# Recorded order for three engines in the middle slots of a deformable bottleneck, two images per statistics instruction, and a norm's scale in two halves

## The chip, the cores and the metric

The kernel runs on one core of a Trainium2 chip. The metric is the device time of one execution in microseconds. Three runs of the kernel before took 2812.07, 2812.46 and 2814.18 us; the median is 2812.46 us.

## What is computed

Two layers follow each other on 64 images of 1024 channels and 14 x 14 pixels. The first is a bottleneck of three convolutions with batch norms. The second, in which the change lies, is a bottleneck whose middle convolution samples its input at learned offsets:

```python
out = conv(x, w1)                                          # 1024 -> 256, 1x1
out = relu(group_norm(out, gn1_scale, gn1_bias))           # 32 groups per image
om = conv(out, w_off, pad=1) + b_off                       # 27 channels, 3x3
off_x, off_y, mask = om[:, :9], om[:, 9:18], sigmoid(om[:, 18:])
sampled = bilinear_sample(out, grid_y + off_y, grid_x + off_x) * mask
out = einsum('bckhw,ock->bohw', sampled, w2)               # 256 -> 256, 9 taps
out = relu(group_norm(out, gn2_scale, gn2_bias))
out = conv(out, w3)                                        # 256 -> 1024, 1x1
out = group_norm(out, gn3_scale, gn3_bias)
return relu(out + x)
```

A group norm takes mean and variance of each image over the pixels and the channels of a group (8 channels in the first two norms, 32 in the third).

## The kernel before, in words

Everything is float32. Channels lie on the 128 partitions, in blocks of 128: 8 blocks of the 1024 channels (`CB`), 2 of the 256 (`MB`). The images are worked on in pairs; a pair's block is a tile of 128 x 392, image 0 in the first 196 columns and image 1 in the last. There are 32 pairs (`NP`).

**Slots.** The second layer is a pipeline over pairs. `slot(t)` (a function inside `build_second_bottleneck`) traces, woven into one list of steps, work on several pairs: `first_conv(t + 1)` (products named d, line 1095), its norm and the offset convolution (om, line 1191) with `selection(t + 1)`, which takes the sigmoid mask (line 1230) and bounces offsets and mask through DRAM; `factors(t + 1)`, the interpolation weights; `transposes(t + 1)`; `sampling(t, e)` (sp, line 1416), bilinear sampling as products with a matrix S, in two halves e of five and four taps; `second_conv(t, e)` (pd, line 1528), 63 products as a sevenfold scheme with sums between them; `second_norm(t - 1)`, `third_conv(t - 1)` (d with 196 columns, line 1665), `third_norm(t - 1)`, and the sum with the input, relu and store, `output`, of pair t - 1's first half of blocks and of pair t - 2's second half. `residual(t + 2)` finishes the first layer's last sum for a later pair. A slot begins with 16 products of `first_conv`; then `sp[0]` is woven with the first half of `third_conv`, then come two of its steps, om and `selection`, then `sp[1]` woven with the rest of `third_conv`, then pd of both halves. Before the first slot `fill` does the work of the first pairs, and after the last `tail` finishes pair 31.

**Who sets the order.** Each engine runs its instructions in the order in which they stand in its stream. With `tc.manual_schedule(engines=...)` an engine's stream is the order of tracing. In the slots before, only TensorE (PE) is in that set. The streams of VectorE (DVE), ScalarE (ACT), GpSimd (POOL) and of the DMA queue on SyncE (SP) are laid by the framework's planner, which picks among what it holds to be ready. An instruction under `tc.keep_in_program_order` stays behind the one traced before it on its engine. The planner also chooses which free buffer a tile gets.

**Buffers.** In PSUM the pool `ps` has three banks (d, transposes), `ps_s` has three (sampled tiles, two tiles of pd), `ps_d` holds `pd0` and `pd1`. A sampled tile `pt` is copied to SBUF by ScalarE (line 1424), which frees its bank. In SBUF, tag `sm0` or `sm1` (one buffer each) holds first X, the factor by columns, and later the sampled taps of the same half. `corners(t, e)` (line 1396) multiplies S by X on VectorE.

**Norms.** `Norm.stats` (line 1004) takes the statistics of a block. BATCH_NORM_STATS2 gives count, mean and sum of squares separately for its even and its odd elements. `total` transposes them, so that channels lie along the free axis, `mean` sums over groups (lines 1025 to 1036), `root` clamps on VectorE (line 1041) and takes the power -0.5 on GpSimd (line 1042), `scale` transposes back (line 1048) and makes the factors `sc` and `sh` (lines 1057 to 1063). `third_norm`'s last step `end` then issues 16 ScalarE activations (line 1733), one for each block and image.

Other lines that the prediction names: 216 and 228, sum and relu of `residual`; 795, a sum of the first layer; 1206 to 1218, the end of the offset convolution (an activation, then sums into `off`); 1257 and 1264, sum and product of `factors`; 1167, four sums of `transform` after a relu (line 1126); 1484, the subtractions between products of pd; 1552 to 1568, `E`, `V` and `h2` at the end of pd; 1672 to 1685, the same for `third_conv`.

Of the kernel before, what the change touches and what calls it, by code (L numbers as in the profile page):

```python
# [10 lines left out]
FP = mybir.dt.float32  # L11
AF = mybir.ActivationFunctionType
# [4 lines left out]
P = 128  # L17
# [3 lines left out]
CB = 8  # L21
# [23 lines left out]
def kernel(  # L45
# [879 lines left out]
    def build_second_bottleneck(l1, path, run, early):  # L925
# [48 lines left out]
        sets = {}  # L974
        for n in (MB, CB):
            sets[n] = [
                one.tile([P, 10 * n + Q], FP, tag=f"st{n}_{m}", name=f"st{n}_{m}_{run}") for m in range(2)
            ]
            for t in sets[n]:
                nc.gpsimd.memset(t, 0.0)  # L980

        class Norm:
# [3 lines left out]

            def __init__(self, nb, size, scol, bcol, name, b0=0):
                self.nb, self.name, self.b0 = nb, name, b0  # L990
                self.scol, self.bcol = scol + b0, bcol + b0
                self.ng, self.n = Q // size, 2 * size
                self.R = None

                kind = MB if nb <= MB else CB
                self.U = 2 * kind
                sets[kind].append(sets[kind].pop(0))
                self.st = sets[kind][-1]
                self.kind = kind

            def stats(self, b, src):
                rows = self.st[:, : 6 * self.U].rearrange("p (s u) -> p s u", s=6)
                for i in range(2):
                    last = nc.vector.bn_stats(rows[:, :, 2 * b + i], src[:, ts(i, HW)])  # L1004
                return last

            def groups(self, v):

                return v.rearrange("p (g n) -> p g n", g=self.ng)

            def total(self):
                self.R = one.tile([P, 2, Q, 2], FP, tag="nR", name=self.name + "R")
                st, U = self.st, self.U
                squares = bass.AP(st.tensor, st.offset + U, [st.ap[0], (3 * U, 2), (U, 2), (1, Q)])
                nc.vector.transpose(self.R.rearrange("p m c e -> p e m c"), squares)

            def mean(self):
                if self.R is None:
                    self.total()
                self.G = small.tile([P, 2, 4], FP, tag="nG", name=self.name + "G")  # L1020
                total, var = (self.G[:, m, : self.ng] for m in range(2))
                D = one.tile([P, 2 * Q], FP, tag="nD", name=self.name + "D")
                means, squares = (self.R[:, m].rearrange("p c e -> p (c e)") for m in range(2))

                nc.vector.tensor_reduce(total, self.groups(means), mybir.AxisListType.X, ALU.add)
                nc.vector.scalar_tensor_tensor(
                    self.groups(D),
                    total.unsqueeze(2).to_broadcast([P, self.ng, self.n]),
                    -1.0 / self.n,
                    self.groups(means),  # L1030
                    ALU.mult,
                    ALU.add,
                )
                nc.vector.tensor_tensor(D, D, D, ALU.mult)
                nc.vector.scalar_tensor_tensor(D, squares, 2.0 / HW, D, ALU.mult, ALU.add)
                nc.vector.tensor_reduce(var, self.groups(D), mybir.AxisListType.X, ALU.add)

            def root(self):

                v = self.G[:, 1, : self.ng]  # L1040
                nc.vector.tensor_scalar(v, v, 0.0, self.n * EPS, ALU.max, ALU.add)
                nc.gpsimd.tensor_tensor(v, v, mhalf[:, : self.ng], ALU.pow)

            def scale(self, tie=lambda v: v):
                nb, U = self.nb, 2 * self.nb
                B = small.tile([P, 2, Q], FP, tag="nB", name=self.name + "B")
                G = self.G[:, :, : self.ng].unsqueeze(3).to_broadcast([P, 2, self.ng, Q // self.ng])
                tie(nc.vector.transpose(B, G))
                self.sc, self.sh = (
                    small.tile([P, self.kind, 2], FP, tag=f"g{v}{self.kind}", name=self.name + v)[:, :nb]  # L1050
                    for v in ("sc", "sh")
                )
                mean, root = (B[:, m, :U].rearrange("p (b i) -> p b i", i=2) for m in range(2))
                gamma, beta = (
                    vec[:, c : c + nb].unsqueeze(2).to_broadcast([P, nb, 2]) for c in (self.scol, self.bcol)
                )
                nc.vector.scalar_tensor_tensor(
                    self.sc, root, self.n**0.5, gamma, ALU.mult, ALU.mult
                )
                nc.vector.scalar_tensor_tensor(  # L1060
                    self.sh, mean, -1.0 / self.n, self.sc, ALU.mult, ALU.mult
                )
                nc.vector.tensor_tensor(self.sh, self.sh, beta, ALU.add)  # L1063
# [558 lines left out]
        def z_of(p, b):  # L1622


            return pairs[p]["z"][b % 2][:, b // 2]
# [94 lines left out]
            order += [(o, c) for o in range(len(first), CB) for c in range(MB)]  # L1720
            return [lambda a=a: step(*a) for a in order]

        def third_norm(p):
            q = pairs[p]

            def end():
                n = q["gn3"][0]

                n.scale(tc.keep_in_program_order)
                for b in (0, 2, 4, 6, 1, 3, 5, 7):  # L1730
                    z = z_of(p, b)
                    for i in range(2):
                        nc.scalar.activation(  # L1733
                            z[:, ts(i, HW)],
                            z[:, ts(i, HW)],
                            AF.Identity,
                            bias=n.sh[:, b, i : i + 1],
                            scale=n.sc[:, b, i : i + 1],
                        )

            return [
                lambda: q["gn3"][0].total(),
                lambda: q["gn3"][0].mean(),
                lambda: q["gn3"][0].root(),
                end,
            ]

        def output(p, m):

# [42 lines left out]
        def weave(a, b):  # L1792

            both = [((n + 0.5) / len(l), m, s) for m, l in enumerate((a, b)) for n, s in enumerate(l)]
            return [s for _, _, s in sorted(both, key=lambda v: v[:2])]
# [19 lines left out]
        def slot(t):  # L1815
# [21 lines left out]
            )  # L1837
            weights = [lambda e=e: corners(t, e) for e in range(2)] if this else []

            late = [lambda: output(t - 2, 1)] if t >= 2 else []  # L1840

            loads = [lambda: load(t + 2)] if t + 2 < NP and not (early and t < 1) else []
            if this and not d1 and not early:
# [61 lines left out]
            todo += put(pd[E - 1], [s for _, s in extra], [k for k, _ in extra])  # L1905
            if ahead:
                todo.append(lambda: list(spread_columns(t + 1, 1)))
            for step in todo:
                step()

# [94 lines left out]
        with tc.manual_schedule(engines={mybir.EngineType.PE}):  # L2005
            if early:
                fill()
            for t in range(0 if early else -2, NP):
                slot(t)
                if t == NP - 2:  # L2010
                    reach()
# [86 lines left out]
```

## Time and profile before

| | |
|---|---|
| median of the runs | 2812.46 us |
| profiled execution | 2814.81 us, its span 2812.9 us |
| granted TensorE clock, mean | 0.992 |
| from 1100 to 2669 us (slots 2 to 29): TensorE busy | 1568.95 of 1569.00 us |
| VectorE, ScalarE, GpSimd busy in it | 1344.76, 933.13, 387.30 us |

The profile has one row per group of instructions: line, engine, operation, what it writes and reads, shapes, the count, then busy time in us and mean duration in ns, then the idle time of the engine before it and what ended it. A timeline has start and duration in us, the engine, and the same names; in brackets is the idle time before and its releaser. In a table by stretches each pair is busy us and, in brackets, the number of instructions, for TensorE's matmuls, its weight loads, VectorE, ScalarE and GpSimd, then the granted clock and the DMAs. Ends of matmuls are modelled, so for TensorE the distance from start to start says more than the duration. The outer parts of the second layer look different from its middle; here is TensorE's share of the time in stretches of 20 us near the end:

```profile
2700.00:2720.00 20.00, 20.00 (x119) 19.15 (x118) 15.11 (x36) 11.55 (x27) 2.71 (x3) 1.00 0.26 76
2720.00:2740.00 20.00, 15.02 (x59) 9.95 (x57) 13.12 (x30) 8.09 (x16) 2.83 (x3) 0.83 0.61 207
2740.00:2760.00 20.00, 18.88 (x89) 14.78 (x90) 11.82 (x32) 8.54 (x21) 6.95 (x12) 1.00 0.13 41
2760.00:2780.00 20.00, 20.00 (x62) 11.59 (x61) 11.94 (x32) 10.64 (x21) 1.57 (x2) 1.00 0.27 80
2780.00:2800.00 20.00, 11.97 (x35) 6.10 (x33) 14.16 (x60) 6.37 (x14) 2.12 (x3) 0.92 0.01 3
```

### The profile page before, as it was taken

How to read it: one execution, taken by the hardware profiler on the slowest of the kernel's cores; microseconds unless marked ns; L12 is line 12 of the kernel's file. 1: busy time of each engine (PE TensorE's matmuls, PEld its weight loads, DVE VectorE, ACT ScalarE, POOL GpSimd, SP SyncE). 2: the span in 40 equal slices, each digit the busy share in tenths (PEclk: the TensorE clock that was granted, in tenths of full speed). 3: DMA queues.
4: the chain of work that ended last, by engine and by line, in shares of the span. 5: the costliest groups of instructions: out<-in, count | busy, mean ns of one | idle time of the engine just before them, and what ended most of it. 6: DMA issues, size and time to landing. Idle time of an engine off the chain costs nothing.

```text
span 2812.9 us, 39819 instructions
## 1 busy us (share of the span) xinstructions
PE 2753.4 (98%) x12930; PEld 2012.7 (72%) x12930; DVE 2372.3 (84%) x5284; ACT 1323.8 (47%) x2723; POOL 936.1 (33%) x1069
## 2 busy tenths in 40 slices
PE   9999899998999989999999999999999999999996
PEld 5555555554555567887888788878887888788874
DVE  7877899998888878888888888888888888888876
ACT  0000221212555545565556555655565556555654
POOL 4630366663666302222221222122212222222221
PEclk9999999999999999999999999999999999999998
DMA  7666000003555544555455545554555455546541
GB/s 229 195 175 172 27 1 0 1 1 131 210 204 212 183 132 149 167 181 192 152 172 177 191 151 177 175 194 146 183 174 192 143 191 167 191 143 193 168 141 52
DMA packets 350318, 424.21 MB, mean 151 GB/s; under 512 B 27892, under 2 KB 292500, under 8 KB 349844
## 3 DMA queue, kind: packets, MB, share of 16 engines
q1 hardware_dynamic: 350100, 421.57, 46.0%
q8 instruction: 104, 1.70, 0.3%
q14 instruction: 114, 0.93, 0.1%
HBM read 296.49 MB, written 116.76 MB: 147 GB/s over the span
## 4 chain that ended last, share of the span: by engine, by line
PE 59%; DVE 2%; DMA 1%; issue 1%; SPq 1%; ACT 0%; POOL 0%; ACTq 0%; POOLq 0%; DVEq 0%
PE pd L1528 22%; PE sp L1416 13%; PE d L1095 10%; PE d L1665 10%; PE om L1191 2%; PE tr L1294 1%; DMA X<-wd 1%; PE pd L1447 1%; DMA S<-wd 0%; DVE st L1004 0%; SPq L1379 0%; SPq L1335 0%; DVE z L1771 0%; DVE S L1396 0%; ACT h L1580 0%
## 5 line engine op out<-in xcount | busy, mean ns | idle before, releaser
L1416 PE MATMUL sp<-S,aT 126*128 126x420 f32 (+3 forms) x1536 | 487.2, 415 | 8.1 <-DVE S L1396 5.6
L1528 PE MATMUL pd<-sm,w2b_sb 128*128 128x196 f32 x2232 | 400.6, 329 | 0.0
L1424 ACT COPY sm<-sp 128x336 f32<-128x336 f32 (+3 forms) x640 | 285.7, 452 | 220.8 <-PE sp L1416 196.9
L1528 PEld LDWEIGHTS pd<-sm,w2b_sb 128*128 128x128 f32 x2232 | 371.3, 190 | 0.0
L534 PE MATMUL c<-v,u_sb 128*128 128x392 f32 x1024 | 343.0, 497 | 10.6 <-DVE bn1sh L167 8.2
L1095 PE MATMUL d<-h,w1b_sb 128*128 128x392 f32 x1024 | 343.9, 493 | 3.9 <-ACT h L228 3.9
L534 PEld LDWEIGHTS c<-v,u_sb 128*128 128x128 f32 x1024 | 194.6, 191 | 159.0 <-DVE v L520 11.7
L1528 PE MATMUL pd<-sm,Sc 128*128 128x196 f32 x1674 | 308.1, 329 | 0.0
L1095 PEld LDWEIGHTS d<-h,w1b_sb 128*128 128x128 f32 x1024 | 193.1, 190 | 140.1 <-ACT h L228 8.0
L1484 DVE TENSOR_TENSOR sm<-sm 128x980 f32<-128x980 f32 (+2 forms) x257 | 268.4, 1055 | 20.1 <-PE pd L1528 8.8
L1528 PEld LDWEIGHTS pd<-sm,Sc 128*128 128x128 f32 x1674 | 278.7, 190 | 0.2
L1416 PEld LDWEIGHTS sp<-S,aT 126*128 126x128 f32 x1536 | 258.4, 191 | 20.9 <-issue 9.7
L1733 ACT ACTIVATE z<-z,gn_0sh,gn_0sc 128x196 f32<-128x196 f32 x496 | 222.5, 537 | 44.6 <-DVE gn_0sh L1063 44.6
L1559 POOL TENSOR_TENSOR E<-V,E 128x196 f32<-128x196 f32 x31 | 18.6, 601 | 543.5 <-DVE V L1558 543.5
L520 DVE TENSOR_TENSOR v<-t 128x392 f32<-128x392 f32 x256 | 193.0, 812 | 0.0
L1665 PE MATMUL d<-h,w3b_sb 128*128 128x196 f32 x744 | 174.0, 329 | 0.8 <-ACT h L1580 0.8
L1665 PEld LDWEIGHTS d<-h,w3b_sb 128*128 128x128 f32 x744 | 133.6, 189 | 51.6 <-issue 19.1
L1758 ACT ACTIVATE z<-z 128x784 f32<-128x784 f32 x124 | 102.7, 853 | 133.0 <-DVE z L1756 132.9
L1677 POOL TENSOR_TENSOR E<-V,E 128x196 f32<-128x196 f32 x124 | 74.2, 598 | 265.5 <-DVE V L1672 265.5
L1396 DVE TENSOR_TENSOR S<-S,X 126x840 f32<-126x840 f32 (+1 forms) x192 | 148.4, 824 | 10.6 <-DMA X<-wd 10.4
L389 PE MATMUL c<-xc,w1a_sb 128*128 128x392 f32 x384 | 149.1, 497 | 5.6 <-DMA xc<-in_x_dram 5.6
L1004 DVE BATCH_NORM_STATS2 st<-z 128x6 f32<-128x196 f32 x496 | 151.6, 352 | 3.2
(684 smaller groups left out, 4967.6 us busy)
## 6 DMA issues: line engine op xcount, KB each, us to landing
xc<-in_x_dram SPq DMA_DIRECT2D x128, 392.0 KB
h<-o SPq DMA_DIRECT2D x64, 784.0 KB
h<-in_x_dram SPq DMA_DIRECT2D x64, 784.0 KB
h<-h SPq DMA_DIRECT2D x64, 784.0 KB
out_dram<-z SPq DMA_DIRECT2D x124, 392.0 KB
X<-wd SPq DMA_DIRECT2D x64, 413.4 KB
S<-wd SPq DMA_DIRECT2D x64, 413.4 KB
S<-wd SPq DMA_DIRECT2D x64, 330.8 KB
```

The costliest lines, as they stand in the source:

```text
L389: nc.tensor.matmul(acc[m], a, b, start=(j == 0), stop=(j == HB - 1))
L520: nc.vector.tensor_tensor(v[:, u].rearrange("p (i y x) -> p i y x", y=7, x=7), cols[c][:, :, i : i + 13 : 2, :], cols[c][:, :, j : j + 13 ...
L534: nc.tensor.matmul(m[u], u_sb[:, c, u, k % 4, ts(o, P)], vts[k][c][:, u], start=(c == 0), stop=(c == MB - 1),)
L1004: last = nc.vector.bn_stats(rows[:, :, 2 * b + i], src[:, ts(i, HW)])
L1095: nc.tensor.matmul(q["pt"][o], w1b_sb[:, c, ts(o, P)], q["y"][:, c, :], start=(c == 0), stop=(c == CB - 1),)
L1396: nc.vector.tensor_tensor(S[:, piece], S[:, piece], X(piece), ALU.mult)
L1416: nc.tensor.matmul(pt[:, i], q["aT"][:, i0 + i, c, starts.index(r0), :], q["S"][e][g, r0][:, :, i0 + i, :], start=(j == 0), stop=(j == len ...
L1424: nc.scalar.copy(dst, pt.rearrange("p i k n -> p k i n"))
L1484: return nc.vector.tensor_tensor(dst, a, b, ALU.subtract)
L1528: nc.tensor.matmul(bank[:, m % 2], a[:, k], b[:, k - k0],  start=(k == 0 and m in (5, 0, 2, 6)), stop=(k == T - 1), skip_group_check=True,)
L1665: nc.tensor.matmul(bank[:, m % 2 if m < 6 else 1], a, b, start=(m < 6), stop=True, skip_group_check=True)
L1733: nc.scalar.activation(z[:, ts(i, HW)], z[:, ts(i, HW)], AF.Identity, bias=n.sh[:, b, i : i + 1], scale=n.sc[:, b, i : i + 1],)
```

## The change

There are three parts. First, slots 2 to 29 (counted from 0) are traced by a new function `steady`, in a block that adds VectorE, GpSimd and ScalarE to the engines in recorded order. SP stays with the planner, and TensorE's order is the one that `slot` gives. Second, `third_norm(p, False)` makes the factors but issues only the eight activations of one half of the blocks; the other eight are issued by `scaled(p, 1)` in the next slot, ahead of `output(p, 1)`. Third, `Norm.stats` takes both images of a block with one instruction, reading their elements alternately, so that even elements are image 0 and odd ones image 1. The layout of sums follows: the groups of both images lie side by side, and in the first two norms (2 blocks of 4 groups) the transpose back is done before the power instead of after it. The third part also holds for the slots outside `steady`, for `fill` and for `tail`.

```diff
             def stats(self, b, src):
                 rows = self.st[:, : 6 * self.U].rearrange("p (s u) -> p s u", s=6)
-                for i in range(2):
-                    last = nc.vector.bn_stats(rows[:, :, 2 * b + i], src[:, ts(i, HW)])
-                return last
+                return nc.vector.bn_stats(rows[:, :, b], src.rearrange("p (i q) -> p q i", i=2))
...
-            def root(self):
-
-                v = self.G[:, 1, : self.ng]
+            def spread(self, tie=lambda v: v):
+                B = small.tile([P, 2, 2, Q], FP, tag="nB", name=self.name + "B")
+                G = self.G[:, :, : 2 * self.ng].unsqueeze(3).to_broadcast([P, 2, 2 * self.ng, self.n])
+                tie(nc.vector.transpose(B, G))
+                self.B = B[:, :, :, : self.nb]
+
+            def root(self, tie=lambda v: v):
+
+
+                if self.nb < self.ng:
+                    self.spread(tie)
+                    v = self.B[:, 1]
+                else:
+                    v = self.G[:, 1:, : 2 * self.ng]
+                half = mhalf[:, : v.shape[1] * v.shape[2]].rearrange("p (a b) -> p a b", a=v.shape[1])
                 nc.vector.tensor_scalar(v, v, 0.0, self.n * EPS, ALU.max, ALU.add)
-                nc.gpsimd.tensor_tensor(v, v, mhalf[:, : self.ng], ALU.pow)
+                nc.gpsimd.tensor_tensor(v, v, half, ALU.pow)
...
-        def third_norm(p):
+        def third_norm(p, both=True):
             q = pairs[p]
 
             def end():
-                n = q["gn3"][0]
-
-                n.scale(tc.keep_in_program_order)
...
+                q["gn3"][0].scale(tc.keep_in_program_order)
+                for m in range(2 if both else 1):
+                    scaled(p, m)
...
+        def scaled(p, m):
+
+            q = pairs[p]
+            n = q["gn3"][0]
+            if m in q.setdefault("scaled", set()):
+                return
+            q["scaled"].add(m)
+            for b in range(m, CB, 2):
+                z = z_of(p, b)
+                for i in range(2):
+                    nc.scalar.activation(
...
-            late = [lambda: output(t - 2, 1)] if t >= 2 else []
+            late = [lambda: scaled(t - 2, 1), lambda: output(t - 2, 1)] if t >= 2 else []
...
+        def steady(t):
+
+
+            sp = [sampling(t, e) for e in range(2)]
+            pd = [second_conv(t, e) for e in range(2)]
+            d1, d3 = first_conv(t + 1), third_conv(t - 1)
+            norm1, norm2, norm3 = first_norm(t + 1), second_norm(t - 1), third_norm(t - 1, False)
+            distances, end = factors(t + 1)
+            half = len(d3) // 2
...
+            todo = at(
+                d1,
+                ((0,), [lambda: scaled(t - 2, 1)]),
+                ((1, 1, 7, 9, 9, 10, 10, 10), norm2),
+                ((6,), [lambda: output(t - 2, 1)]),
+                ((10,), [lambda: corners(t, 0)]),
+            )
+            todo += at(weave(sp[0], d3[:half]), ((4, 4, 8, 14, 16, 18, 21), norm1))
+            todo += [lambda: corners(t, 1)] + d3[half : half + 2]
+            todo += offset_conv(t + 1) + selection(t + 1) + [lambda: load(t + 2)]
+            todo += weave(sp[1], d3[half + 2 :])
+            todo += at(
+                pd[0],
+                ((1, 1, 1, 9), norm3),
+                ((5, 20), [lambda e=e: first_sum(t, e) for e in range(2)]),
+                ((6, 11, 16, 21), transposes(t + 1)),
+                ((6, 13), [distances, end]),
+                ((21,), [lambda: residual(t + 2)]),
+            )
+            todo += [lambda: list(spread_rows(t + 1, 0)), lambda: list(spread_columns(t + 1, 0))]
+            todo += [lambda: list(spread_rows(t + 1, 1)), lambda: lend(t + 1)]
+            todo += at(pd[1], ((16,), [lambda: output(t - 1, 0)]))
+            todo.append(lambda: list(spread_columns(t + 1, 1)))
+            for step in todo:
+                step()
...
-            for t in range(0 if early else -2, NP):
+            middle = range(2, NP - 2) if early else range(0)
+            for t in range(0 if early else -2, middle.start):
+                slot(t)
+            with tc.manual_schedule(
+                engines={
+                    mybir.EngineType.DVE,
+                    mybir.EngineType.Pool,
+                    mybir.EngineType.Activation,
+                }
+            ):
+                for t in middle:
+                    steady(t)
+            for t in range(middle.stop, NP):
                 slot(t)
```

In `at(steps, (places, extras), ...)` an extra step is traced just ahead of the step with the given number.

## The prediction

> **What bounds the kernel now.** I read the page's busy row first, then the busy time by stretches over the slots that the change rewrites (slot t starts with the first product of `first_conv(t + 1)`, line 1095; slots 2 to 29 run from about 1100 to 2669 us), then TensorE's waits, then the timeline of one slot, the one that starts at 1828.6 us.
>
> ```profile
> PE 2753.4 (98%) x12930; PEld 2012.7 (72%) x12930; DVE 2372.3 (84%) x5284; ACT 1323.8 (47%) x2723; POOL 936.1 (33%) x1069
> ```
>
> ```profile
> 1100.00:2669.00 1569.00, 1568.95 (x8902) 1295.98 (x8901) 1344.76 (x3304) 933.13 (x1986) 387.30 (x532) 1.00 0.53 173
> ```
>
> The second line is the stretch of the 28 slots, and TensorE (the first pair of numbers in it) is busy in it for 1568.95 of 1569.00 us at the full granted clock. Asked for the stretch from 1156 to 2669 us, the table of waits has not one row for PE; VectorE has 86%. The starts of slots are 56.04 to 56.07 us apart (56.35 the first time). Busy could still hide slack, so I looked at start to start: a 196-column product takes two records 0.166 us apart wherever it stands. The slots are bound by TensorE's own instructions. The change keeps their number and order (`steady` weaves d1, sp, d3, om, transposes and pd as `slot` does), so it can shorten nothing there. It can only open gaps, or move something at the edges (fill, slots 0, 1, 30, 31, tail), where TensorE does wait.
>
> **The parts, one by one.**
>
> Statistics: per slot 24 BATCH_NORM_STATS2 on 196 elements become 12 on 392, whose two images are read alternately, 784 bytes apart.
>
> ```profile
> L1004 DVE BATCH_NORM_STATS2 st<-z 128x6 f32<-128x196 f32 x496 | 151.6, 352 | 3.2
> ...
> L586 DVE BATCH_NORM_STATS2 st<-h 128x6 f32<-128x392 f32 x64 | 34.6, 555 | 0.0
> ```
>
> The old ones follow each other every 0.27 us, so a block costs 0.54. A contiguous 392 takes 0.555 us, and as neighbours overlap by about 0.08, it costs 0.475. Gain 0.07 x 12 = 0.8 us of VectorE a slot, off the path. [...] But line 216 reads its operand `r` in just this way (two streams alternately, also 784 bytes apart) and takes 623 ns, where line 795, also three operands of 392, without the jump, takes 625. I take the row: 0.555. [...]
>
> Norm: the transpose in `spread` handles 128 instead of 64 elements, 312 instead of 238 ns by lines 1015 and 1048: +0.075 x 3 = 0.2 us a slot. `root` and `scale` trade places of the transpose; the count of instructions stays. POOL's power works on 4 or 2 values as against 4 or 1 (1.0 to 1.7 us whatever the number). Together with the statistics nothing for the tail: -0.07 and +0.075 on a chain.
>
> Third norm's scale in halves: 16 activations at 0.44 us apart become 8 in pd and 8 at the next slot's start. ScalarE reaches `E` (line 1552) at once after its product instead of behind them and the residual. The waits say what that frees:
>
> ```profile
> DVE V L1558 <- ACT E L1552: 51.1, 27, 1.9
> ```
>
> 1.9 us a slot of VectorE's waiting goes, so the second norm is 2 us early. Nobody on TensorE waited for it: gain 0. Next in line is then TensorE itself.
>
> The recorded order: this decides. The planner had moved three things freely; now ScalarE, VectorE and GpSimd each run in the order in which `steady` emits. ScalarE gets the mask (line 1230, in `selection`) before all copies of sampled tiles of `sp[1]`. In the trace before, it stands after three of them:
>
> ```profile
> 1853.48 0.42 ACT L1206 ACTIVATE om<-om,boff_sb 32x196 f32<-32x196 f32 x1 [1.53 <-PE om L1191]
> 1854.59 0.44 ACT L1424 COPY sm<-sp 128x336 f32<-128x336 f32 x1 [0.69 <-PE sp L1416]
> 1855.44 0.44 ACT L1424 COPY sm<-sp 128x336 f32<-128x336 f32 x1 [0.42 <-PE sp L1416]
> 1856.34 0.44 ACT L1424 COPY sm<-sp 128x336 f32<-128x336 f32 x1 [0.46 <-PE sp L1416]
> 1857.96 0.53 ACT L1230 ACTIVATE mask<-off 32x392 f32<-32x392 f32 x1 [1.18 <-DVE off L1218]
> ```
>
> The mask waits for VectorE's `off`. Behind it now queue the copies, and they empty the three banks of pool `ps_s`. TensorE's sampling products start here:
>
> ```profile
> 1853.77 0.73 PE L1416 MATMUL sp<-S,aT 126*128 126x336 f32 x2
> ...
> 1854.68 0.73 PE L1416 MATMUL sp<-S,aT 126*128 126x336 f32 x2
> ...
> 1855.58 0.73 PE L1416 MATMUL sp<-S,aT 126*128 126x336 f32 x2
> ...
> 1856.48 0.73 PE L1416 MATMUL sp<-S,aT 126*128 126x336 f32 x2
> ```
>
> Three banks take the first three (pd's two tiles of this pool are long free); the fourth, due at 1856.48, needs the first one's copy done. When does that come? I lay VectorE's recorded order behind the point that ScalarE's paced relus leave unchanged:
>
> ```profile
> 1848.03 1.13 DVE L1167 TENSOR_TENSOR X<-a 128x168 f32<-128x168 f32 x4 [0.19 <-ACT a L1126]
> 1849.08 0.56 DVE L1672 TENSOR_TENSOR V<-d,E 128x392 f32<-128x392 f32 x1
> ...
> 1852.27 1.92 DVE L1396 TENSOR_TENSOR S<-S,X 126x672 f32<-126x672 f32 x3
> ...
> 1856.54 1.38 DVE L1218 TENSOR_TENSOR off<-om,om 32x84 f32<-32x84 f32 x6
> ```
>
> Start to start: four transform sums to 1849.08; V 0.48, 1849.56; two statistics of d3's first block (the planner had done them at 1846.4) 0.95, 1850.51; the second transform (its relu ended at 1850.33) 1.11, 1851.62; line 1681's sum 0.48, 1852.10; line 1685's 0.27, 1852.37; `corners(t, 1)` 1.84, 1854.21; line 1207 0.28, 1854.49; line 1208 0.33, then line 1218 six times from 1854.86, ending at 1856.24 (before: 1857.92; the planner had put four statistics and a V between). The mask runs 1856.27 to 1856.80, the copy starts 0.09 earlier and ends at 1857.15, and after a semaphore the product runs 0.04 later (43 ns in PE's other waits of this kind): 1857.19. **TensorE waits 1857.19 - 1856.48 = 0.71 us, in each of 28 slots: 19.9 us.** The later copies are 0.44 apart against products 0.9 apart, so the queue recovers at once.
>
> [...]
>
> Bounds of this term: if VectorE had no backlog at all, lines 1207 to 1218 could start on ScalarE's 1853.90, and the copy ends at 1856.86, a wait of 0.42 us (11.8 us in sum). [...] Below nothing it can't go: TensorE has no idle time to give back.
>
> VectorE in pd, by the same adding: `first_sum(t, 0)` stands behind the third norm's mean and root and would end at 1867.27, its user (line 1528 with Sc) starts at 1868.28; the subtraction after product 6 moves behind the `wt` sum (line 1257) and ends at 1869.25, needed at 1870.16; the next, behind the norm's scale, ends at 1871.3 and is needed at 1872.04; the last 1872.9 and 1873.7. Margins 0.7 to 1.0 us: cost 0, but the cover is thin. Transposes' copies wait behind the eight scales until about 1874; their readers are next slot's products, and the fourth transpose needs the first copy only. GpSimd's sums keep their order.
>
> DMAs: `steady` issues the same ones; SP's queue stays planned. `off` and the mask come 1.7 us earlier, so `wt`, `wd`, S and X do too; output of half 0 starts about 4 us earlier and shares the queue with S and X. `corners(t, 0)` had its last landing at 10.2 us into this slot (8.4 in the next) and must be done by about 13, since the first sample's copy overwrites X and the fourth sample (14.5) needs that copy: cost 0.
>
> **Sum.** The profiled execution took 2814.81 us (span 2812.9), 2.35 above the median of the runs, 2812.46. The added 19.9 us go on either: 2834.7 on the profiled one, 2832.4 on the median; I say 2832.
>
> **Rivals.**
> 1. The wait does not come (0.17): 2812, not slower. `off` would have to end 0.71 us earlier than my sum, before 1855.53, or the copies be planned ahead of the mask. For it: VectorE had slack at 1847 to 1848, and my 0.71 is a difference of long sums. Against: even without backlog 0.42 stays. That the nested order doesn't bind ScalarE (the change not doing what it says) belongs here.
> [...]
> 3. Faster at the edges (0.08): PE idles 2617 + 2119 ns at 2728 and 2732 us, on S and X of the last slot and on line 1561; another SP order there could return up to 5 us, and the fill's gaps another few, if the middle is free: 2804 to 2808.
>
> **Numbers.** The wait alone, 0.62: 2822 to 2845 (0.4 to 1.1 us a slot). The range 2810 to 2850 adds most of rival 1 and the start of rival 2. A difference of under 0.2% (5.6 us) is what a measurement of this kernel can hardly tell from none. Slower: 0.62 + 0.13 = 0.75; same: most of rival 1, 0.16; faster 0.09.
>
> **What would show it.** Slots 56.7 to 56.9 us apart; in PE's waits a row "sp L1416 <- ACT sm" of 0.6 to 0.8 us, some 28 times; the mask directly behind line 1206's activation, ScalarE idle about 2.3 us between them; BATCH_NORM_STATS2 on 392 at 0.55; no wait of V for E. I am wrong if PE's rows in the middle stay empty, if the waits sit in pd, or if the statistics take 0.9 us.

## The result, and the profile after

The kernel after takes 2844.82 us (median of four runs, 2844.26 to 2844.94); the kernel before took 2812.65 us beside it (2812.07 to 2814.18). The ratio is 1.0113, with a 95% interval of 1.0096 to 1.0131: 32.2 us slower. The prediction said 2832, range 2810 to 2850. (The two profiled executions, 2844.26 and 2814.81 us, lie 29.5 apart; the account below is of these two.) In the new file the lines have moved down: the copies of sampled tiles are line 1438 (1424 before), the mask is 1244 (1230), the sampling products 1430 (1416), `V` in `third_conv` 1686 (1672).

The profiled execution after has a span of 2842.5 us against 2812.9, at the same mean clock of 0.992. By places: what comes before slot 2 is 0.3 us shorter, the slots 2 to 29 are 31.4 us longer (57.18 us apart instead of 56.05), and what follows the start of slot 30 is 1.5 us shorter (142.0 against 143.5). So everything to be explained lies in the 28 slots. From the page of after, the row of busy times and the group of the sampling products (behind the bar busy us, mean ns, then the idle time in front and its main releaser):

```profile
PE 2754.5 (97%) x12930; PEld 2013.2 (71%) x12930; DVE 2379.2 (84%) x4900; ACT 1333.6 (47%) x2723; POOL 950.3 (33%) x1069
...
L1430 PE MATMUL sp<-S,aT 126*128 126x420 f32 (+3 forms) x1536 | 488.6, 416 | 36.8 <-ACT sm L1438 28.5
```

TensorE is busy as long as before (2754.5 against 2753.4 us), and its share fell. The missing time is idle time ahead of line 1430. In the table of waits of after (us in total, times, longest) it is the largest row of TensorE; between 1156 and 2700 us it is the only one (27.1 us, 27 times), where before there was none:

```profile
PE sp L1430 <- ACT sm L1438: 28.5, 29, 1.1
```

One slot shows where it comes from. ScalarE's timeline of after, at the slot that starts at 1842.8 us:

```profile
1867.54 0.41 ACT L1220 ACTIVATE om<-om,boff_sb 32x196 f32<-32x196 f32 x1 [0.47 <-PE om L1205]
1870.80 0.53 ACT L1244 ACTIVATE mask<-off 32x392 f32<-32x392 f32 x1 [2.85 <-DVE off L1232]
1871.24 1.07 ACT L1438 COPY sm<-sp 128x336 f32<-128x336 f32 x3
```

ScalarE stands still for 2.85 us in front of the mask, and then three copies come at once: they had been ready. TensorE's timeline of after, same slot:

```profile
1869.64 0.73 PE L1430 MATMUL sp<-S,aT 126*128 126x336 f32 x2
1870.21 0.50 PE L1679 MATMUL d<-h,Sb 128*128 128x196 f32 x2
1871.70 0.83 PE L1430 MATMUL sp<-S,aT 126*128 126x336 f32 x2 [1.00 <-ACT sm L1438]
```

Samples come every 0.90 us; the fourth was due at 1870.54 and came at 1871.70, when the first copy had ended: 1.16 us late. The pair of products then lasts 0.83 instead of 0.73, another 0.10: from the start of the first product after the wait to that of the second 388 ns pass, where the neighbouring pairs have 286. Together 1.26 us. That is more than the 1.13 by which the slots grew; the difference is a second thing, found below.

### The profile page after: what moved, and what is told of

It is laid out like the page before. It is cut to its first block, busy times and chain, and to the rows that moved or that the text cites. A ratio compares the mean times of both kernels' runs of the same rounds, so it can differ in the third digit from the quotient of the medians.

```text
span 2842.5 us, 39446 instructions
## 1 busy us (share of the span) xinstructions
PE 2754.5 (97%) x12930; PEld 2013.2 (71%) x12930; DVE 2379.2 (84%) x4900; ACT 1333.6 (47%) x2723; POOL 950.3 (33%) x1069
## 4 chain that ended last, share of the span: by engine, by line
PE 47%; DVE 11%; ACT 3%; issue 2%; DMA 1%; POOL 0%; SPq 0%; DVEq 0%; ACTq 0%; POOLq 0%
PE pd L1542 21%; PE d L1109 10%; PE sp L1430 8%; PE d L1679 6%; DVE X L1181 2%; DVE S L1410 2%; DVE off L1232 1%; DVE z L1695 1%; DVE st L1005 1%; ACT a L1140 1%; DMA X<-wd 1%; PE tr L1308 1%; ACT sm L1438 1%; PE pd L1461 1%; DVE V L1686 1%
## 5 line engine op out<-in xcount | busy, mean ns | idle before, releaser
L1410 DVE TENSOR_TENSOR S<-S,X 126x840 f32<-126x840 f32 (+1 forms) x192 | 159.3, 880 | 11.1 <-DMA X<-wd 10.1
L216 DVE SCALAR_TENSOR_TENSOR h<-h,bn3sc,h 128x392 f32<-128x392 f32 x256 | 141.0, 620 | 0.0
```

What stands on the lines that cost most here:

```text
L216: return nc.vector.scalar_tensor_tensor(y,  r[:, b, :].rearrange("p (b r x) -> p r x b", x=7, b=2), bn3.sc[:, b : b + 1], y, ALU.mult, ALU ...
L1410: nc.vector.tensor_tensor(S[:, piece], S[:, piece], X(piece), ALU.mult)
```

## The experiments

Slot distances are from the profile of each run. All kernels but `e10` and `e11` are the kernel after with one or a few edits.

**Is it the mask's place?** The first kernel leaves all streams recorded and emits only the mask (with its transfers) later, behind three copies.

```diff
-            todo += offset_conv(t + 1) + selection(t + 1) + [lambda: load(t + 2)]
-            todo += weave(sp[1], d3[half + 2 :])
+            largest, chosen = selection(t + 1, True)
+            todo += offset_conv(t + 1) + [largest]
+            todo += at(weave(sp[1], d3[half + 2 :]), ((6, 6), [chosen, lambda: load(t + 2)]))
```

> All of the change, but the mask's activation (with its transfers and the loads behind them) is emitted after the third sample's copy of the second half instead of right behind the offset convolution; VectorE's order and its maximum stay where they are. Theory (the mask at the head of ScalarE's queue holds up the first sample's copy, and so the bank that the fourth sample needs): no wait of PE sp for ACT sm is left in slots 2 to 29, slots 56.05 to 56.1 us apart, 2811 to 2814 us. Rival (VectorE's recorded order is late as a whole, and the mask is only where it shows): its order is unchanged, so 0.4 us or more a slot stays, in sp or in pd: 2823 us or more.

Measured: 2836.22 us against 2815.21, ratio 1.0073 (1.0057 to 1.009); slots 56.91 us apart. The row "sp waits for sm" is gone from the middle, but only about a quarter of the loss went with it; the expected 2811 to 2814 us did not come, and the rival's "2823 or more" did. Another wait took its place; the waits of this kernel between 1100 and 2660 us, where `V` is line 1691, and then TensorE's timeline:

```profile
PE d L1684 <- DVE V L1691: 19.9, 27, 0.8
```

```profile
1866.14 0.73 PE L1435 MATMUL sp<-S,aT 126*128 126x336 f32 x2
1867.61 0.60 PE L1684 MATMUL d<-T,w3b_sb 128*128 128x196 f32 x2 [0.74 <-DVE V L1691]
```

The waiting product is the seventh of a block of `third_conv`, half a microsecond further on in the stream. It adds to the PSUM bank that `V` reads, and starts when `V` is done (here `V` ends at 1867.56 us, the product starts at 1867.61); and VectorE's recorded order has `V` behind the six sums of `off` and the maximum (line 1248 in after). This wait was there in the kernel after too, behind the other: there `V` ends at 1871.95 us, and the product follows at 1872.37, which the late fourth sample had delayed already. Of these two waits only the longer one costs: a slot of after falls behind at the fourth sample alone.

**Do the statistics of the first block carry the delay?** They stand ahead of the second transform in my sum, 0.95 us. This kernel takes those of block 0 earlier.

```diff
-                    stats(before[j])
+                    if before[j] != early:
+                        stats(before[j])
...
-                    if j == order[-1]:
+                    if j in (order[-1], early):
                         stats(j)
...
-            d1, d3 = first_conv(t + 1), third_conv(t - 1)
+            d1, d3 = first_conv(t + 1), third_conv(t - 1, 0)
```

> All of the change, but the statistics of the third convolution's first block are emitted after its last sum instead of inside the next block, that is in VectorE's idle stretch 17 to 19 us into the slot: 2 instructions, 0.96 us, leave the chain that ends in off. Theory (the wait is VectorE's chain up to off, then mask, then copy, less TensorE's time): the wait falls from 1.12 to about 0.17 us a slot, 2817 to 2820 us. Rival (the place of the mask costs by itself, whatever VectorE does before it): 2844 us, unchanged.

Measured: 2845.68 us in one run, slots 57.24 us apart: no gain, as the rival said. VectorE's timeline of this kernel, and then GpSimd's:

```profile
1864.90 1.65 DVE L1181 TENSOR_TENSOR X<-a 128x168 f32<-128x168 f32 x4 [0.72 <-ACT a L1140]
```

```profile
1864.88 0.60 POOL L1691 TENSOR_TENSOR z<-V 128x196 f32<-128x196 f32 x1
```

The transform (line 1181) now starts when its relu has ended, 0.16 us earlier in the slot than in after, but its first sum takes 0.79 us instead of 0.56 and ends 0.07 later. What decides is GpSimd: its sum of line 1691 is still running when VectorE's sum starts, and VectorE's sum ends 0.20 us after GpSimd's has ended. So it is in all 28 slots of after and of `e8` (below) and in 27 here, to within 0.02 us, whether VectorE's sum starts 0.26, 0.36 or 0.59 us before that end. In the 28th, slot 2, VectorE's sum starts first, by 0.02 us: it takes 0.34 us, and it is GpSimd's that ends late, 0.47 us after it. In the chain of sums I had counted the statistics, which are not on the path, and not GpSimd, which is.

**Which engine's order costs?** Two single runs leave engines out of the recorded set: in the first ScalarE goes back to the planner, in the second VectorE and GpSimd do.

```diff
                 engines={
                     mybir.EngineType.DVE,
                     mybir.EngineType.Pool,
-                    mybir.EngineType.Activation,
                 }
```

> All of the change, but ScalarE's stream in slots 2 to 29 is the planner's again; VectorE and GpSimd keep the recorded order. Theory (mask first on ScalarE): the planner puts copies ahead of the mask, 2811 to 2816 us. Rival (VectorE's recorded order): 2838 us or more.

```diff
                 engines={
-                    mybir.EngineType.DVE,
-                    mybir.EngineType.Pool,
                     mybir.EngineType.Activation,
                 }
```

> All of the change, but only ScalarE keeps the recorded order in slots 2 to 29; VectorE and GpSimd are the planner's. Theory: the mask still stands ahead of the copies; off ended at 29.3 us of the slot in the planner's order of before and at 28.0 in the recorded one, so the wait is between 0.7 and 2.5 us a slot, 2832 to 2882 us. Rival (VectorE's recorded order): 2812 us.

Measured: 2836.28 us with ScalarE free, slots 56.91 apart, the same wait for `V` as with the mask moved by hand: the planner puts the mask behind two copies. Neither the expected 2811 to 2816 nor the rival's 2838 came. With ScalarE alone recorded, 2889.36 us, above the 2882 that I had allowed. From the waits and from ScalarE's timeline of that kernel:

```profile
PE sp L1430 <- ACT sm L1438: 63.2, 29, 2.3
```

```profile
1422.68 0.53 ACT L1244 ACTIVATE mask<-off 32x392 f32<-32x392 f32 x1 [4.09 <-DVE off L1232]
```

The wait is over 2 us a slot instead of 1, since a planned VectorE makes `off` later still: the slots are 58.41 us apart, 2.5 more than a slot free of waits (55.91, below), the top of what I had allowed. But seven of them, mostly each fourth or fifth, take about 1.7 us more (60.07 to 60.08, the first 60.32). Here is one of them, by stretches:

```profile
1451.85:1483.21 31.36, 29.11 (x157) 20.15 (x157) 26.35 (x67) 16.50 (x36) 11.31 (x16) 1.00 0.36 119
1483.21:1486.62 3.41, 3.41 (x15) 3.41 (x14) 0.94 (x2) 1.28 (x4) 0.00 (x0) 0.50 0.46 142
```

For 3.41 us the granted clock (third number from the end) is 0.50, beginning 1.2 us after the wait of 2.25 us has ended; 3.41 us at half speed are 1.7 us lost. All seven long slots have one such stretch, no other of the 28 has one, and none stands in these slots of any other kernel here, where the waits stay at about 1.2 us or less. Why the clock falls in seven slots and not in the 21 others with the same wait no run separates.

**How much is VectorE's backlog, how much the mask's place itself?** Here the multiplication of `corners(t, 1)` comes earlier, so that VectorE is idle when the offset convolution ends.

```diff
+                ((14,), [lambda: corners(t, 1)]),
             )
-            todo += [lambda: corners(t, 1)] + d3[half : half + 2]
+            todo += d3[half : half + 2]
```

> All of the change, but corners(t, 1), 1.84 us of VectorE, is emitted ahead of step 14 of the weave of sp[0], into VectorE's idle stretch 17 to 19 us into the slot, instead of behind the weave. Theory (two waits, both behind VectorE's queue that begins with the second transform at 21.6 us: the mask's, and the seventh product's for V, whose bank it adds to): off ends 1.84 us earlier, at about 26.1, the first sample's copy at 27.0 before 27.74, V at 27.3 before 28.3; both waits go though the mask keeps its place; as before the change within 0.1%, slots 56.05 to 56.1 us apart. Rival (the mask's place or the recorded order costs by itself): 0.7% above before or more.

Measured: 2828.18 us against 2813.98, ratio 1.0047 (1.003 to 1.0064); slots 56.55 us apart. ScalarE's timeline of this kernel, and TensorE's wait in it between 1100 and 2660 us:

```profile
1859.54 0.41 ACT L1220 ACTIVATE om<-om,boff_sb 32x196 f32<-32x196 f32 x1 [0.47 <-PE om L1205]
1862.18 0.53 ACT L1244 ACTIVATE mask<-off 32x392 f32<-32x392 f32 x1 [2.23 <-DVE off L1232]
```

```profile
PE sp L1430 <- ACT sm L1438: 10.6, 28, 0.4
```

Neither expectation came: the wait stays, at half its size. From the end of line 1220 to the mask 2.23 us pass with VectorE waiting for nothing else: that is the eight sums. The fourth sample comes 0.53 us late, and with its longer record the slot loses 0.63. (The row gives less, 0.4, since it counts from the modelled end of the product before.) So half of the 1.26 us is the mask ahead of the copies, and half is what stood ahead of `off` on VectorE.

**Is the wait for `V` all that is left?** The next kernel moves the mask as the first did, and emits lines 1221 to 1232, the sums into `off`, and the maximum later too, so that `V` comes first.

```diff
+            largest, chosen = selection(t + 1, True)
+            ends = []
-            todo += offset_conv(t + 1) + selection(t + 1) + [lambda: load(t + 2)]
-            todo += weave(sp[1], d3[half + 2 :])
+            todo += offset_conv(t + 1, ends)
+            todo += at(
+                weave(sp[1], d3[half + 2 :]),
+                ((3, 6, 6, 10), [lambda: ends[0](), chosen, lambda: load(t + 2), largest]),
+            )
```

> As e1 (mask after the third copy), and the eight VectorE sums that end the offset convolution and its maximum are emitted behind V of the next block instead of ahead of it. Theory (the 0.85 us a slot that e1 left are the seventh product's wait for V): V ends at 26.4 instead of 29.2, the wait goes, and at most 0.2 us a slot come back where the block's sums are now later; 0 to 0.2% above before. Rival (VectorE is late as a whole in this stretch): the wait moves on to the next block's products, 0.5% above before or more.

Measured: 2823.6 us against 2813.98, ratio 1.0035 (1.0023 to 1.0048); slots 56.50 us apart. The wait for `V` is gone, and another has come, as the rival said, at a smaller cost than it said; the waits of this kernel between 1100 and 2660 us, `z` being line 1707:

```profile
PE d L1691 <- DVE z L1707: 9.4, 28, 0.3
```

The sum of line 1707 frees the bank for the next block, and is late because VectorE does the sums of `off` in between, where this edit put them. It costs 0.59 us a slot.

**Does the recorded order cost anything when its order is good?** Kernel `e9` joins two edits that helped, the mask behind three copies (`e1`) and `corners(t, 1)` early (`e5`), and moves the maximum, but not the sums of `off`, behind `V`.

```diff
+                ((14,), [lambda: corners(t, 1)]),
             )
-            todo += [lambda: corners(t, 1)] + d3[half : half + 2]
-            todo += offset_conv(t + 1) + selection(t + 1) + [lambda: load(t + 2)]
-            todo += weave(sp[1], d3[half + 2 :])
+            todo += d3[half : half + 2]
+            largest, chosen = selection(t + 1, True)
+            todo += offset_conv(t + 1)
+            todo += at(
+                weave(sp[1], d3[half + 2 :]),
+                ((3, 6, 6), [largest, chosen, lambda: load(t + 2)]),
+            )
```

> The change with its recorded order, mended in three places: mask after the third copy (e1), corners(t, 1) in VectorE's idle stretch (e5), the maximum behind V of the next block. Theory (two waits, and no third): V ends near 27.9 us of the slot, before the seventh product at 28.3; no PE wait in slots 2 to 29, slots 55.90 to 55.95 us apart as in e7, 0.1 to 0.35% below before. Rival (the recorded order has further waits behind these): slots over 56.1 us apart, above before.

Measured: 2808.4 us against 2812.74, ratio 0.9984 (0.9975 to 0.9993); slots 55.91 us apart, and no row for TensorE in the table of waits between 1156 and 2660 us. ScalarE's timeline of this kernel, with the mask (here line 1254) where the planner had it:

```profile
1849.73 0.41 ACT L1220 ACTIVATE om<-om,boff_sb 32x196 f32<-32x196 f32 x1 [0.46 <-PE om L1205]
1850.84 0.44 ACT L1443 COPY sm<-sp 128x336 f32<-128x336 f32 x1 [0.69 <-PE sp L1435]
1851.69 0.44 ACT L1443 COPY sm<-sp 128x336 f32<-128x336 f32 x1 [0.42 <-PE sp L1435]
1852.60 0.44 ACT L1443 COPY sm<-sp 128x336 f32<-128x336 f32 x1 [0.46 <-PE sp L1435]
1852.93 0.52 ACT L1254 ACTIVATE mask<-off 32x392 f32<-32x392 f32 x1
```

The mask waits for nothing there and delays nobody. All of the loss is thus a matter of three places in the order; recording as such costs nothing that can be seen. But the slots are now 0.14 us *shorter* than before, which by my prediction could not be.

**Where do the 0.14 us come from?** Two kernels go back to the planner for all slots and keep the rest of the change. The first keeps the new norm and the scale in halves:

```diff
-                part(back, third_norm, t - 1),
+                part(back, third_norm, t - 1, not 2 <= t < NP - 2),
...
-            middle = range(2, NP - 2) if early else range(0)
-            for t in range(0 if early else -2, middle.start):
+            middle = range(0)
+            for t in range(0 if early else -2, 0):
                 slot(t)
```

> The change without the recorded order: all slots are traced by slot and planned, with the statistics of two images at once and the third norm's scale in two halves in slots 2 to 29. Theory (the recorded order alone costs): as before within 0.15%. Rival (strided statistics or the split scale cost): 0.3% or more above before.

Measured: 2807.32 us against 2813.98, ratio 0.9977 (0.9968 to 0.9987), slots 55.91 us apart: below the 0.15% that I had allowed, and the lowest ratio here, though its interval overlaps that of `e9`. The second puts the old norm into the kernel after, with its recorded order.

```diff
-                return nc.vector.bn_stats(rows[:, :, b], src.rearrange("p (i q) -> p q i", i=2))
+                for i in range(2):
+                    last = nc.vector.bn_stats(rows[:, :, 2 * b + i], src[:, ts(i, HW)])
+                return last
```

(and `total`, `mean`, `root` and `scale` with it.)

> The recorded order and the scale in halves, with the norm and its statistics as they were before (two instructions of 196 a block). Theory: 4 instructions 0.27 us apart end 0.12 us later than 2 of 0.48 ahead of the second transform, which they already end just behind; 2844 to 2849 us. Rival (the strided statistics are what slows VectorE's chain): 2835 us or less.

Measured: 2842.46 us in one run, slots 57.17 us apart, as with the new norm: in the recorded order the statistics neither cost nor bring anything that this shows. The last two kernels split the gain. They are the kernel before, first with the new `Norm` alone:

```diff
-                for i in range(2):
-                    last = nc.vector.bn_stats(rows[:, :, 2 * b + i], src[:, ts(i, HW)])
-                return last
+                return nc.vector.bn_stats(rows[:, :, b], src.rearrange("p (i q) -> p q i", i=2))
...
-            def root(self):
+            def root(self, tie=lambda v: v):
```

> The kernel before with the statistics of two images at once and nothing else of the change. Theory (the 0.146 us a slot that e7 gained at the product with the second sum T comes from the scale in halves): slots 56.03 to 56.07 us apart, before within 0.1%. Rival (the shorter statistics bring the second norm forward): 55.95 us apart or less, 0.15% below before.

And with the old norm and the scale in halves alone:

```diff
+                for m in range(2 if both else 1):
+                    scaled(p, m)
...
-                part(back, third_norm, t - 1),
+                part(back, third_norm, t - 1, not 2 <= t < NP - 2),
...
-            late = [lambda: output(t - 2, 1)] if t >= 2 else []
+            late = [lambda: scaled(t - 2, 1), lambda: output(t - 2, 1)] if t >= 2 else []
```

> The kernel before with the third norm's scale in two halves in slots 2 to 29 and nothing else of the change. Theory: V no longer waits for E, the second norm and with it GpSimd's sums T come about 1 us earlier, the product with the second sum starts on time: slots 55.90 to 55.95 us apart, 0.1 to 0.3% below before. Rival (e7's gain is the statistics'): slots 56.03 us apart or more, before within 0.1%.

Measured: the new norm alone takes 2814.69 us against 2812.74, ratio 1.0005 (0.9996 to 1.0014), slots 56.12 us apart; the halves alone 2809.8, ratio 0.9989 (0.998 to 0.9998), slots 55.91 us apart. So the gain is the scale in halves. The new norm alone even makes a slot 0.07 us longer, a little more than I had expected: the product behind GpSimd's sum still comes late, and some 5.5 us further on another one waits, in the table of waits of the queue of weight loads (PEld) between 1156 and 2660 us:

```profile
PEld d L1679 <- DVE z L1695: 14.8, 27, 0.9
```

What the halves take away is in the kernel before, in the same table, which the prediction had not drawn on:

```profile
PEld d L1665 <- POOL T L1597: 15.0, 27, 0.6
```

Between 1156 and 2660 us it waits 27 times, 15.0 us in all; in the kernel with the halves the row is absent. GpSimd's and TensorE's timelines of the kernel before show what the row means:

```profile
1839.92 1.27 POOL L1597 TENSOR_TENSOR T<-h,T 128x196 f32<-128x196 f32 x1
```

```profile
1840.16 0.50 PE L1665 MATMUL d<-T,Sb 128*128 128x196 f32 x2
1840.50 0.87 PE L1416 MATMUL sp<-S,aT 126*128 126x420 f32 x2
1841.25 0.60 PE L1665 MATMUL d<-T,Sb 128*128 128x196 f32 x2
```

GpSimd's sum ends at 1841.19 us and the product that needs it begins at 1841.25. It has no bracket (no idle time in front), for the modelled end of the sampling product covers the gap; but it comes 0.04 us late and its pair lasts 0.60 instead of 0.50. TensorE was "busy" and waited. In the kernel with the halves six of the 16 activations stand behind `E` (line 1552): ScalarE copies it 2.34 us before the slot begins (1825.88 us) instead of 0.30 after. GpSimd's sum takes 1.27 us there too, but ends 1.10 us before its product starts, and the pair lasts 0.50. ScalarE's, GpSimd's and TensorE's timelines of that kernel:

```profile
1823.54 0.46 ACT L1552 COPY E<-pd 128x392 f32<-128x392 f32 x1
```

```profile
1836.13 1.27 POOL L1597 TENSOR_TENSOR T<-h,T 128x196 f32<-128x196 f32 x1
```

```profile
1838.50 0.50 PE L1665 MATMUL d<-T,Sb 128*128 128x196 f32 x2
```

The page of the kernel with the halves shows it in the sum:

```profile
PE 2747.7 (98%) x12930; PEld 2015.0 (72%) x12930; DVE 2374.2 (85%) x5284; ACT 1336.7 (48%) x2723; POOL 937.0 (33%) x1069
```

The same 12930 products are busy for 2747.7 us instead of 2753.4. Of these 5.7 us, 28 times 0.146, or 4.1, are the wait found here; the rest was not traced.

That closes the account of the 28 slots. Free of these waits a slot takes 55.91 us. Before it took 0.146 more; after, that is gone and 1.26 are added: 1.26 - 0.146 = 1.11 net, 31.2 us in 28 slots, against 31.4 measured. Laid beside a slot of the kernel with the halves, product by product, a slot of after falls behind at the fourth sample (1.16 and 0.10 us) and nowhere else, one of before at the product behind GpSimd's sum (0.04 and 0.10) and nowhere else, and one of `e9` or `e7` nowhere.

## Why the prediction was right, and where its numbers were not

**The main step held.** The mask went ahead of the copies on ScalarE, the fourth sample waits for the first copy, once in each of the 28 slots. My sum assumed that no copy on ScalarE goes past the waiting mask. After shows it, in the slot that starts at 1842.8 us: by the modelled ends the first three samples were done at 1868.57, 1869.47 and 1870.37 us, ScalarE stood still from 1867.95 until the mask began at 1870.80, and the copies came at 1871.24. Rival 1 (no wait) fell, and no wait came in pd: a slot falls behind at this one place and nowhere in pd, so the margins of 0.7 to 1.0 us were enough. That the time lies inside 2822 to 2845 us was partly luck: the wait of 1.26 us a slot is over the 1.1 that I had allowed, and a gain of 0.146 that I had put at nothing brought the net to 1.11. The signs that I had named were off in the same way: slots 57.18 us apart instead of 56.7 to 56.9, a row of 1.0 us instead of 0.6 to 0.8, ScalarE idle 2.85 us instead of 2.3.

**Its size was 0.71 us a slot and measured 1.26.** The mis-sized term is my sum of VectorE's work from the relu to the end of `off`. VectorE's timeline of after, the same slot:

```profile
1864.58 1.42 DVE L1181 TENSOR_TENSOR X<-a 128x168 f32<-128x168 f32 x4
1865.92 0.55 DVE L1695 TENSOR_TENSOR z<-d,E 128x392 f32<-128x392 f32 x1
1866.40 0.34 DVE L1699 TENSOR_TENSOR z<-d,V 128x196 f32<-128x196 f32 x1
1866.66 1.91 DVE L1410 TENSOR_TENSOR S<-S,X 126x672 f32<-126x672 f32 x3
1868.61 0.35 DVE L1221 TENSOR_TENSOR om<-om,om 32x196 f32<-32x196 f32 x1
1869.00 0.35 DVE L1222 TENSOR_TENSOR om<-om,om 32x196 f32<-32x196 f32 x1
1869.38 1.39 DVE L1232 TENSOR_TENSOR off<-om,om 32x84 f32<-32x84 f32 x6
```

I had put the second transform at 1.11 from start to start; it takes 1.34, because GpSimd's sum holds up its first sum, as shown with `e2`; in before, the planner had it start 0.04 to 0.05 us before that sum of GpSimd ended, and it took 0.33 us. GpSimd's timeline of after:

```profile
1864.34 0.60 POOL L1691 TENSOR_TENSOR z<-V 128x196 f32<-128x196 f32 x1
```

It ends at 1864.94, and VectorE's first sum at 1865.14. I had further let the sum of line 1221 begin 0.08 before `corners` ends; it begins 0.04 after (1.95 from start to start instead of 1.84), though it uses nothing of `corners`, and no run separates why. And I had let the sum of line 1222 begin before that of 1221 ends; but 1222 overwrites what 1221 reads, and it begins 0.04 after its end (0.39 instead of 0.28). That is 0.23 + 0.11 + 0.11 = 0.45 us. The second missing term is 0.10, the longer pair of a product that has waited. 0.71 + 0.45 + 0.10 = 1.26. (The chain starts 0.13 us earlier in the slot than I had it, and the fourth sample is due 0.14 earlier, so these two cancel.)

**The lower bound was low by the last two of these terms.** With an idle VectorE I said 0.42; `e5` measured 0.53, about the 0.11 more for line 1222, and 0.63 with the longer pair.

**The statistics cost about what I said.** They read two images alternately. The view of line 1005 in after (durations are minimum, median and maximum):

```profile
L1005 DVE BATCH_NORM_STATS2 st<-z x248: 548/567/585, 1067.6 to 2789.0; 128x6 f32<-128x392 f32 x124
```

0.567 us against the 0.555 that I took from the contiguous block of line 586 in before, 0.012 more; to go by the row of line 216 was right. The chance of 0.13 for a longer time, and the range above 2845 us, stood on slower statistics and on waits in pd. No run shows either: the statistics took these 0.567 us, and in no table of waits does TensorE wait in pd in the 28 slots. The 0.95 of statistics in my chain, however, wasn't binding, as `e2` and `e8` showed.

**"It can shorten nothing there" was wrong.** I took busy time as proof that TensorE waited for nothing, and checked it by one distance, 0.166 us, "wherever it stands". Behind GpSimd's sum, in the very slot of the timeline, the two records stand 0.270 us apart. The step costed at nothing, the scale in halves, gives 0.146 us a slot. That ScalarE reaches `E` earlier was right, and the wait of `V` for `E` went as said; the error was "nobody on TensorE waited for it". The gain hid in the loss: it is 4.1 us in 28 slots.

**One wait was missed.** The product that adds to the bank which `V` reads would have cost 0.98 to 1.00 us a slot by itself. In the change it cost nothing, because the mask's wait lies just ahead and is longer.

**Edges:** rival 3's up to 5 us came as 1.5 at the end, and 0.3 at the start; what gave them was not traced.

What stays open: `e7` is 6.7 us below the kernel before beside it, of which 4.1 are the hidden wait; in the profiles the rest lies before slot 2 and behind the start of slot 30, and I haven't traced it. Open too is what made the clock fall in only seven slots of `e4`.

## What to carry to other kernels

In a stream laid by hand, place an instruction with a late input behind everything that is ready and that another engine needs, and look for the next wait behind the one you remove: here two lay within a microsecond and only the longer showed, and moving work to remove the second made a third. "Busy 100%" is not "waits for nothing": look at the weight loads' waits, and compare the same product's duration and distance at all its places in the stream. In a chain of sums, add start to start only where such a pair stands in the trace, and lay the other engines' sums that run at the same time beside it.

## What was not expected of the hardware

In these runs a product that has waited costs about 0.10 us beyond the wait: the pair lasts 0.83 instead of 0.73 us (sampling), or 0.60 instead of 0.50 (`third_conv`), whether it came 0.04 us late (before) or 2.4 (`e4`). A pair of 0.60 also follows the last of the narrow offset products, so the length alone doesn't prove a wait.

GpSimd's sum of two 128 x 196 tiles takes 0.60 us at one place and 1.27 us at another of the same slot, with the same shape. The traces show the difference: at the slow places VectorE is multiplying S by X (`corners`) when GpSimd's sum begins, and GpSimd's sum ends 0.46 us after that multiplication. In before it is this one, ending at 1840.73 us, where GpSimd's sum ends at 1841.19:

```profile
1837.99 2.74 DVE L1396 TENSOR_TENSOR S<-S,X 126x840 f32<-126x840 f32 x3
```

So it is in all slots 2 to 29 of all kernels here: GpSimd's sums ahead of `third_conv` that begin within such a multiplication end 0.45 to 0.47 us after it, whether that makes them 0.66 us long or 1.40, and those that don't take 0.59 to 0.61. The other way round, in after VectorE's first sum of the second transform ended 0.20 us after the GpSimd sum that it met. An engine off the critical path thus set both the wait that the kernel before had (0.146 us a slot) and the largest of the terms that the prediction's sum lacked (0.23).
